# Eight residual sums held behind their written place, one addition per unit in the last batch, and the stores of routed rows sent one table after the other

## The chip, the cores and the metric

The kernel runs on one core of a Trainium2 chip. The core has four compute engines that each work through a queue of their own in order: TensorE (PE in the profile) multiplies matrices, VectorE (DVE) and ScalarE (ACT) work elementwise, GpSimd (POOL) adds and starts indirect transfers; SyncE (SP) starts the other transfers. The engines meet through semaphores. The metric is the device time of one execution in microseconds (us), and lower is better.

## The reference

Four blocks follow each other, each added to the residual `x` of 4 batches by 512 rows by 256 columns (fp32):

```python
x = x + _L0_xattn_ref(ctx_1024, _layernorm(x), ...)    # 8 heads of 128, keys: 1601 context rows and the 512 latents
x = x + _L0_ffn_ref(_layernorm(x), ...)                # 8 experts, top 2, capacity 512 rows per expert
x = x + _L1_xattn_ref(ctx_1024, _layernorm(x), ...)    # 8 heads of 32, keys: 1601 context rows, softmax
x = x + _L1_ffn_ref(_layernorm(x), W1, b1, W2, b2, Wr, br)

def _L1_ffn_ref(x, W1, b1, W2, b2, Wr, br):            # 8 experts, top 2, no capacity
    logits = xf @ Wr + br
    topv, _ = lax.top_k(logits, TOPK)
    masked = jnp.where(logits >= topv[:, TOPK - 1:TOPK], logits, -jnp.inf)
    weights = jax.nn.softmax(masked, axis=-1)
    h = gelu(jnp.einsum('td,edh->eth', xf, W1) + b1[:, None, :])
    expert_out = jnp.einsum('eth,ehd->etd', h, W2) + b2[:, None, :]
    return jnp.einsum('etd,te->td', expert_out, weights)
```

The softmax of the second attention needs, for each query and head, the sum of its 1601 exponentials. The last block routes each row to two of eight experts.

## The kernel before

The four blocks are four stages on the time line. The first attention ends at about 1600 us, the first FFN at 1883, the second attention at 2416, and the second FFN at the end of the span.

**The order of work.** Instructions are written in one program, and a scheduler orders each engine's queue by its own priorities, unless the program ties it: `tc.keep_in_program_order(instruction)` ties one instruction to its written place in its engine's queue, and `in_order(*computing)` ties all of PE, VectorE, ScalarE and GpSimd. The whole second attention is tied so (line 1753); the end of the first FFN is not.

**The end of the first FFN.** It works in two halves of eight experts (`all_experts`). Beside the second half, `keys_next` projects the context of batch 1 to the keys and values of the second attention: PE writes `ps_k` (L1166) and `ps_v` (L1182), and VectorE and ScalarE copy them to the tile `kv` in turn (`evacuate`, L122 and L124). After the ninth of these steps `add_collected(0, got0)` adds the FFN's results to `x` of batch 0: GpSimd has fetched eight tiles `g` of 128x256 from the table `slot_y` by indirect transfers (L360), and VectorE adds each, times its share (L382). The layer norm of batch 0 (statistics L143 and L144) follows. Here the scheduler chose the order: all eight sums and the statistics stand in VectorE's queue ahead of the copy of the last 65 columns of keys, "L122 kv<-ps_k 128x65".

**The second attention.** It has 16 units: four batches, two groups of four heads (`o`), two halves of 256 queries (`f`); units 12 to 15 are the last batch. A unit has seven steps (`PER_UNIT`) of 256 keys, the last one shorter. A global step (0 to 111) takes these in turn: `weights` of this step (PE L1538 and L1548, then four exponentials by ScalarE, L1562, into two tiles `pT` of 128x1024); then, for the step before, `weigh` (PE L1581 multiplies `pT` by the values), `add_weights`, the `maxima` of the next unit (PE L1281, VectorE's reduction "tops" L1292, in seven rotating PSUM banks that `weights` uses too), and `total`. Sums of exponentials are made in one of two ways. For a step in `ADDED = (1, 3, 5)` VectorE adds its two tiles to those of step 0 (L1571), and at the last step PE multiplies these sums by ones (L1600). For the other steps PE multiplies `pT` itself by ones in `total` (L1600, 16 matmuls). At the end of a unit, `closing` scales the outcome (VectorE, L1628 and L1630, to the tile `got`, of which there is one) and GpSimd adds it to `x` (L1637).

**Routing for the second FFN.** While batch b+1 is in the attention, `route2(b)` (L440 to L617) prepares batch b for the last stage, cut into pieces that are put at fixed steps (`routed`, `last_routed`): the layer norm, the tile `pay` (four tiles of 128 normalised rows with their number and shares; for batches 0 to 2 GpSimd writes it, L455 and L463, and there is one such tile), its transposes by PE (L194), the router's logits, the two experts of each row and the places of its rows. There are two tables in the chip's memory: `rows_a` holds the first G = 256 rows of each expert among batches 0 to 2, `rows_b` all that come after. A row whose place is in the other table is given a place out of bounds, which the transfer drops. So every tile of 128 rows is sent four times: for each of its two experts (k) to `rows_a` and to `rows_b`, by indirect stores of GpSimd (`scatters`, L591): 16 stores per batch, alternating between the tables, two at a time, at steps 56 to 63 for batch 0, 84 to 91 for batch 1, and 105 to 111 for batch 2. Batch 3, which has only the eight stores to `rows_b`, is routed in the last stage. Stores to the same table are ordered by a semaphore: the next one waits until the one before has landed. The pay of batch 2 is at step 92, its transposes at steps 93 and 94.

**The start of the second FFN.** At step 109 SP loads the first expert's rows from `rows_a` to `cw` (`load_first_rows`, L1677); at step 111 PE transposes them (`turn_first`, L1483), and the first expert's first layer follows (L1492). Then come, in the last stage, the layer norm of batch 3 (L143), which needs all additions to `x`, the load of the second expert's rows (L1829), their transposes (L1483), VectorE's copy of these (L1484) and the second expert's matmuls (L1492).

Of the kernel before, what the change touches and what calls it, by code (L numbers as in the profile page):

```python
# [11 lines left out]
AF = mybir.ActivationFunctionType  # L12
ALU = mybir.AluOpType
# [5 lines left out]
B, S, D = 4, 512, 256  # L19
M = 1601  # L20
NT = S // P
# [27 lines left out]
NOWHERE = 65536.0  # L49
PER_UNIT = -(-NM // 2)  # L50
ADDED = (1, 3, 5)

# [28 lines left out]
def xattn_ffn_twice(ctx: ExitStack, tc: tile.TileContext, a: dict, out: bass.AP):  # L83
    nc = tc.nc
# [128 lines left out]
    rows_a = dram.tile([E * G, PAY], F32, name="rows_a")  # L213
    rows_b = dram.tile([ROWS + G, PAY], F32, name="rows_b")
# [154 lines left out]

        return got, [lambda t=t, k=k: one_of(t, k) for t in range(NT) for k in range(2)]  # L370

    def add_collected(b, got, tiles=range(NT), by=None):
        for t in tiles:
            for k in range(2):
                j = b * NT + t
                xs = x[b][:, t, :]
                g, share = got[2 * t + k], prob[k][:, j : j + 1]
                if by:
                    by.tensor_scalar(g, g, share, None, ALU.mult)
                    by.tensor_tensor(xs, xs, g, ALU.add)  # L380
                else:
                    nc.vector.scalar_tensor_tensor(xs, g, share, xs, ALU.mult, ALU.add)  # L382


    lane_i = brief.tile([P, 1], I32, name="lane_i")
# [18 lines left out]
    place_a = [const.tile([P, NX], I32, name=f"place_a{k}") for k in range(2)]  # L404
    place_b = [const.tile([P, NX], I32, name=f"place_b{k}") for k in range(2)]
# [31 lines left out]
    def route2(b, two, psum, tag, first=0, n=NT):  # L437

        by = nc.vector if b == B - 1 else nc.gpsimd
# [144 lines left out]
        def scatters():  # L584

            sent = 0
            for k in range(2):
                for t in range(n):
                    for rows, at in ((rows_a, place_a), (rows_b, place_b))[b == B - 1 :]:
                        j = b * NT + first + t  # L590
                        nc.gpsimd.indirect_dma_start(  # L591
                            out=rows[:, :],
                            out_offset=bass.IndirectOffsetOnAxis(ap=at[k][:, j : j + 1], axis=0),
                            in_=pay[:, t, :],
                            in_offset=None,
                            bounds_check=E * G - 1 if rows is rows_a else ROWS - 1,
                            oob_is_err=False,
                        )
                        sent += 1
                        if sent % 2 == 0:  # L600
                            yield

        sending = scatters()
        for t0 in range(0, n, 2):
            ps = psum.tile([P, 2, D], F32, tag=tag, name="ps_b2")
            for k in range(2):
                t = t0 + k
# [3 lines left out]
            xs = xb[:, t0 : t0 + 2, :]  # L611
# [6 lines left out]
        yield from sending  # L618


    banks, tags = {}, {}

    def slots(of, e, half, n=CT):
# [705 lines left out]
    with ExitStack() as st:  # L1329
# [117 lines left out]
        def keys_next():  # L1447
            *kv, steps = keys_values(ps_s, "s", 1)
            kvs.append(kv)
            steps[9:9] = [lambda: add_collected(0, got0)]  # L1450
            steps = iter(steps)
            asking = queries(0, qTs)

            for few, asks in ((4, 0), (5, 0), (3, 1), (0, 1), (2, 1), (0, 1), (1, 1), (1, 1), (0, 1)):
                for _ in range(few):
                    next(steps)()
                for _ in range(asks):
                    next(asking)
                yield
            assert next(steps, None) is None  # L1460

            firsts = [(0, g) for g in range(len(pieces))] + [(1, g) for g in range(3)]
            for k, (u, g) in enumerate(firsts):
                maxima(u, g)
                if (u, g) == (0, len(pieces) - 1):
                    negated(0)
                yield
                if k == 0:
                    next(asking)
                    assert next(asking, None) is None  # L1470
                if (u, g) == (1, 0):
                    to_row(0)
                if k % 2 == 0:
                    yield
# [34 lines left out]
    with ExitStack() as st:  # L1509
# [20 lines left out]
        def weights(u, s):  # L1530

            b, o, f = units[u]
            js = keys_of(s)
            r, n = rows_of(js[-1], NM, TAIL), len(js) * QH
            pss = [ps_s.tile([P, 512], F32, tag="s", name=f"ps_w{i}") for i in range(HG)]
            for i in range(HG):
                rows = slice(i * DH1, i * DH1 + 2 * PARTS)
                nc.tensor.matmul(  # L1538
                    pss[i][:r, :n].rearrange("p (k q) -> p k q", q=QH),
                    lhsT=ones_b[rows, :r],  # L1540
                    rhs=below[u % 2][rows, :].unsqueeze(1).to_broadcast([2 * PARTS, len(js), QH]),
                    start=True,
                    stop=False,
                )
            for k, j in enumerate(js):
                for i in range(HG):
                    rows = slice(i * DH1, (i + 1) * DH1)
                    nc.tensor.matmul(  # L1548
                        pss[i][:r, k * QH : (k + 1) * QH],
                        lhsT=kvs[b][0][o][rows, j * P : j * P + r],  # L1550
                        rhs=qTs[b][rows, o, f * QH : (f + 1) * QH],
                        start=False,
                        stop=k == len(js) - 1,
                    )
            pTs = []
            for h in range(2):
                if s == 0:
                    pT = two.tile([P, 2, 512], F32, tag=f"sum{h}", name=f"sum{h}")
                else:
                    pT = some.tile([P, 2, 512], F32, tag="pT", name="pT")  # L1560
                for i in range(2):
                    nc.scalar.activation(pT[:r, i, :n], pss[2 * h + i][:r, :n], AF.Exp)  # L1562
                pTs.append(pT)
            if s == 0:
                sums[u] = pTs
            return pTs

        def add_weights(u, s, pTs):
            if s in ADDED:
                for to, pT in zip(sums[u], pTs):  # L1570
                    nc.vector.tensor_tensor(to, to, pT, ALU.add)  # L1571

# [16 lines left out]

        def total(u, s, pTs, ps):  # L1590

            of = [(s, pTs)] if s and s not in ADDED else []
            if s == PER_UNIT - 1:
                of.append((0, sums.pop(u)))
            for s0, tiles in of:
                js = keys_of(s0)
                r = rows_of(js[-1], NM, TAIL)
                for k in range(len(js)):
                    for i in range(HG):
                        nc.tensor.matmul(  # L1600
                            ps[i * DH1 : (i + 1) * DH1, QH:],
                            lhsT=ones[:r, :DH1],
                            rhs=tiles[i // 2][:r, i % 2, k * QH : (k + 1) * QH],
                            start=False,
                            stop=s0 == 0 and k == 1,
                            skip_group_check=True,
                        )
# [601 lines left out]
```

## Time and profile before

| quantity | value |
|---|---|
| median of 3 runs | 2722.71 us (2721.53, 2722.71, 2730.08) |
| the profiled execution | 2712.06 us, its span 2710.2 us |
| mean granted clock of TensorE | 0.991 |
| end of the exponentials (L1562) of step 56, 59 | 2160.18, 2176.15 us |
| of step 84, 86, 91 | 2298.61, 2307.96, 2331.05 us |
| of step 105, 107, 111 | 2397.29, 2404.45, 2414.20 us |
| start of unit 12, 13, 14, 15 | 2293.48, 2325.92, 2360.19, 2393.93 us |
| landing of the last store of batch 0, 1, 2 | 2193.30, 2330.86, 2423.76 us |
| half of TensorE's clock granted | 1750.19 to 1760.43, 2378.24 to 2388.48 us |

The span runs from the first to the last instruction of the profiled execution, and all times of the profile count from its start. The execution's own time has 1.9 us more than the span. The lines of the profile read: start, length, engine, line of the program, operation, output from inputs with their shapes, how many instructions are put together, and in square brackets the idle time of the engine before it and what ended it. A store's length on GpSimd (about 1 us) is that of issuing it; its landing is later, 2.07 to 3.72 us after its start for those whose landing the trace has in the second attention.

### The profile page before, as it was taken

How to read it: one execution, taken by the hardware profiler on the slowest of the kernel's cores; microseconds unless marked ns; L12 is line 12 of the kernel's file. 1: busy time of each engine (PE TensorE's matmuls, PEld its weight loads, DVE VectorE, ACT ScalarE, POOL GpSimd, SP SyncE). 2: the span in 40 equal slices, each digit the busy share in tenths (PEclk: the TensorE clock that was granted, in tenths of full speed). 3: DMA queues.
4: the chain of work that ended last, by engine and by line, in shares of the span. 5: the costliest groups of instructions: out<-in, count | busy, mean ns of one | idle time of the engine just before them, and what ended most of it. 6: DMA issues, size and time to landing. Idle time of an engine off the chain costs nothing. (4 is left out here: it accounts for less than half of the span.)

```text
span 2710.2 us, 38196 instructions
## 1 busy us (share of the span) xinstructions
PE 2636.0 (97%) x14620; PEld 1790.7 (66%) x14620; DVE 1364.6 (50%) x2461; ACT 917.9 (34%) x1577; POOL 356.9 (13%) x372
## 2 busy tenths in 40 slices
PE   6999999999999999999999999899999999999997
PEld 3666676666666666767666678777454454468887
DVE  6544556644456544455454441124777878853111
ACT  4332234333334233333333221122444444452221
POOL 0000000100000100000100000101441431322542
PEclk9999999999999999999999999999999999999999
DMA  5444434433443443433343455543433100025672
GB/s 178 111 113 121 99 90 113 105 93 89 108 112 84 115 98 85 99 95 87 98 104 95 124 184 166 177 156 99 125 123 122 64 30 7 20 98 180 202 222 78
DMA packets 191323, 302.89 MB, mean 112 GB/s; under 512 B 41783, under 2 KB 113272, under 8 KB 188440
## 3 DMA queue, kind: packets, MB, share of 16 engines
q1 hardware_dynamic: 152392, 218.33, 29.0%
q0 software_dynamic: 14160, 46.31, 5.8%
q10 hardware_dynamic: 24576, 35.68, 5.2%
q8 instruction: 118, 1.93, 0.3%
q14 instruction: 77, 0.63, 0.1%
HBM read 111.46 MB, written 51.07 MB: 60 GB/s over the span
## 5 line engine op out<-in xcount | busy, mean ns | idle before, releaser
L949 DVE TENSOR_REDUCE top<-ps_s 128x1 f32<-128x2113 f32 x128 | 301.7, 2357 | 584.1 <-PE ps_s L941 584.1
L978 PE MATMUL ps_o<-pT,v 128*128 128x256 f32 x2176 | 519.4, 380 | 0.0
L941 PE MATMUL ps_s<-kT,qT 128*128 128x512 f32 (+1 forms) x1280 | 489.1, 526 | 6.3 <-ACT attn L955 6.3
L978 PEld LDWEIGHTS ps_o<-pT,v 128*128 128x128 f32 x2176 | 407.9, 190 | 110.5 <-issue 65.4
L955 ACT ACTIVATE attn<-ps_s,top 128x2113 f32<-128x2113 f32 x128 | 259.0, 2024 | 478.4 <-DVE top L949 458.8
L941 PEld LDWEIGHTS ps_s<-kT,qT 128*128 128x128 f32 x1280 | 241.8, 190 | 252.1 <-issue 236.0
L970 DVE STREAM_TRANSPOSE pT<-swapped 128x2176 f32<-128x2176 f32 x128 | 312.3, 2440 | 32.8 <-DMA swapped<-attn 23.4
L1292 DVE TENSOR_REDUCE tops<-ps_s 128x1 f32<-128x512 f32 (+2 forms) x428 | 251.1, 648 | 120.0 <-PE ps_s L1281 120.0
L887 PE MATMUL ps_k<-kvin,wkv 128*128 128x512 f32 (+2 forms) x640 | 259.4, 528 | 3.4 <-DVE kvin L807 2.9
L924 PE MATMUL ps_v<-wkv,kvin 128*128 128x256 f32 x1088 | 255.3, 381 | 1.9 <-ACT v L931 1.4
L924 PEld LDWEIGHTS ps_v<-wkv,kvin 128*128 128x128 f32 x1088 | 204.8, 190 | 38.3 <-issue 6.0
L1562 ACT ACTIVATE pT<-ps_w 128x512 f32<-128x512 f32 (+1 forms) x384 | 184.2, 565 | 130.9 <-PE ps_w L1548 130.8
L903 ACT ACTIVATE kT<-ps_k,bqk 128x512 f32<-128x512 f32 (+1 forms) x192 | 100.9, 555 | 259.6 <-PE ps_k L887 136.0
L887 PEld LDWEIGHTS ps_k<-kvin,wkv 128*128 128x128 f32 x640 | 115.8, 191 | 75.4 <-issue 64.0
L931 ACT COPY v<-ps_v 128x512 f32<-128x512 f32 x144 | 80.0, 560 | 213.2 <-PE ps_v L924 135.9
L1281 PE MATMUL ps_s<-kv,qT 32*128 32x512 f32 (+1 forms) x1024 | 128.4, 556 | 2.8 <-DVE got L1630 2.5
L1548 PE MATMUL ps_w<-qT,kv 32*128 32x256 f32 (+1 forms) x1664 | 119.2, 384 | 0.0
L1571 DVE TENSOR_TENSOR sum<-sum,pT 128x1024 f32<-128x1024 f32 x96 | 114.8, 1237 | 6.0 <-ACT pT L1562 6.0
L654 PE MATMUL ps_h<-sxT,w 128*128 128x256 f32 (+1 forms) x512 | 108.0, 367 | 4.0 <-DVE sxT L644 2.5
L741 POOL TENSOR_TENSOR x<-x,bo 128x256 f32<-128x256 f32 x16 | 11.7, 761 | 743.8 <-DVE lat L181 545.8
L1345 PE MATMUL ps_y<-w,hT 128*128 128x256 f32 x480 | 108.7, 382 | 0.0
L654 PEld LDWEIGHTS ps_h<-sxT,w 128*128 128x128 f32 x512 | 91.8, 190 | 21.1 <-issue 4.2
(317 smaller groups left out, 2763.0 us busy)
## 6 DMA issues: line engine op xcount, KB each, us to landing
swapped<-attn SPq DMA_DIRECT2D x1536, 68.0 KB, 2.1
swapped<-attn ACTq DMA_DIRECT2D x512, 68.0 KB, 2.3
w<-in_w_dram SPq DMA_DIRECT2D x32, 1024.0 KB, 5.8
rows_b<-empty SPq DMA_DIRECT2D x36, 530.0 KB, 4.6
w_e<-in_wall_dram SPq DMA_DIRECT2D x5, 2052.0 KB, 11.2
cw<-in_ctxT_dram SPq DMA_DIRECT2D x4, 1601.0 KB
ctx_b<-in_ctx_dram SPq DMA_DIRECT2D x3, 1536.0 KB, 7.6
slot_x<-scrap SPq DMA_DIRECT2D x8, 512.0 KB, 3.3
```

What stands on the lines that cost most here:

```text
L654: nc.tensor.matmul(ps[:, f, :], lhsT=w1[:, c, (f0 + f) * P : (f0 + f + 1) * P], rhs=sxT[:, c, :], start=c == 0, stop=c == DC - 1,)
L887: nc.tensor.matmul(ps[:, :n], lhsT=wkv[:, c, hs], rhs=kvin[:, c, : n // 32, k, :] if k < 4 else flat_kvin[c][:, left : left + P], start=c ...
L924: nc.tensor.matmul(ps[:, k, :], lhsT=flat_kvin[c][:, j * P : (j + 1) * P], rhs=wkv[:, c, cols], start=c == 0, stop=c == DC - 1,)
L941: nc.tensor.matmul(flat[:, j0 : j0 + n], lhsT=qT[:, t * P : (t + 1) * P], rhs=kT[:, j0 : j0 + n], start=True, stop=True,)
L949: nc.vector.tensor_reduce(top, flat[:, :L], AX.X, ALU.max, negate=True)
L955: nc.scalar.activation(attn[:, :L], flat[:, :L], AF.Exp, bias=top, accum_out=total)
L970: nc.vector.transpose(pT[:, :, k * P : (k + 1) * P].rearrange("p c (a i) -> p a c i", a=4), swapped.rearrange("p a (c i) -> p a c i", i=32),)
L978: nc.tensor.matmul(ps, lhsT=v[:, j - parts[part][0], (h % 2) * DH0 : (h % 2 + 1) * DH0], rhs=pT[:, j, :], start=j == 0, stop=j == NB - 1,)
L1281: nc.tensor.matmul(pss[i][:, at : at + n], lhsT=qTs[b][rows, o, q0 : q0 + P], rhs=kvs[b][0][o][rows, j0 : j0 + n], start=True, stop=True,)
L1292: nc.vector.tensor_reduce(tops[u][:, t : t + at // n, some, j0 // 512], of, AX.X, ALU.max,)
L1548: nc.tensor.matmul(pss[i][:r, k * QH : (k + 1) * QH], lhsT=kvs[b][0][o][rows, j * P : j * P + r], rhs=qTs[b][rows, o, f * QH : (f + 1) * Q ...
L1562: nc.scalar.activation(pT[:r, i, :n], pss[2 * h + i][:r, :n], AF.Exp)
```

## The change

It has three parts.

The eight sums of `add_collected(0, got0)` are tied to their written order (`behind=True`). In the changed order VectorE has the copy of the 65 columns of keys, two copies `sxT` of the FFN and the first two copies of values ahead of the first sum; seven sums stand ahead of the third copy of values.

For the units of the last batch the steps whose `pT` VectorE adds are `ADDED_LATE = (3,)`. Sixteen additions of 128x1024 leave VectorE's queue (steps 1 and 5 of four units), and eight blocks of matmuls with ones (L1600) join PE's.

The stores of a batch go to `rows_a` first, all eight, and then to `rows_b`, at the same steps as before. Each store has another wait: for the last exponential of the step in which it is written (`latest[0]`). On GpSimd's queue the addition L1637 of the unit that closes among the stores stands after the sixth store of `rows_a` for batches 0 and 1, and after the eighth for batch 2. SP's load of the first expert's rows, which stood behind the sixth store of batch 2 to `rows_a` with the last two held until it had ended, now stands behind the eighth.

```diff
@@ -49,6 +49,7 @@
 ADDED = (1, 3, 5)
+ADDED_LATE = (3,)
@@ add_collected @@
-    def add_collected(b, got, tiles=range(NT), by=None):
+    def add_collected(b, got, tiles=range(NT), by=None, behind=False):
 ...
-                    nc.vector.scalar_tensor_tensor(xs, g, share, xs, ALU.mult, ALU.add)
+                    summed = nc.vector.scalar_tensor_tensor(xs, g, share, xs, ALU.mult, ALU.add)
+                    if behind:
+                        tc.keep_in_program_order(summed)
@@ route2, scatters @@
-            for k in range(2):
-                for t in range(n):
-                    for rows, at in ((rows_a, place_a), (rows_b, place_b))[b == B - 1 :]:
+            for rows, at in ((rows_a, place_a), (rows_b, place_b))[b == B - 1 :]:
+                for k in range(2):
+                    for t in range(n):
                         j = b * NT + first + t
-                        nc.gpsimd.indirect_dma_start(
+                        store = nc.gpsimd.indirect_dma_start(
 ...
+                        tc.add_manual_dep(
+                            store.ins,
+                            latest[0].ins.name,
+                            mybir.DependencyInfo(
+                                mybir.DependencyClass.Sync, mybir.DependencyReason.DATA
+                            ),
+                            reason="paced",
                         )
                         sent += 1
@@ before the stages @@
+    latest = []
@@ keys_next @@
-            steps[9:9] = [lambda: add_collected(0, got0)]
+            steps[9:9] = [lambda: add_collected(0, got0, behind=True)]
@@ weights @@
-                    nc.scalar.activation(pT[:r, i, :n], pss[2 * h + i][:r, :n], AF.Exp)
+                    latest[:] = [
+                        nc.scalar.activation(pT[:r, i, :n], pss[2 * h + i][:r, :n], AF.Exp)
+                    ]
@@ add_weights and total @@
+        def added(u):
+            return ADDED if units[u][0] < B - 1 else ADDED_LATE
+
-            if s in ADDED:
+            if s in added(u):
 ...
-            of = [(s, pTs)] if s and s not in ADDED else []
+            of = [(s, pTs)] if s and s not in added(u) else []
```

More of the change, by code (lines that the diff above doesn't have):

```diff
@@ L597, in scatters @@
                             oob_is_err=False,
+                        )
+                        tc.add_manual_dep(
[5 more added lines that the diff above has]
+                            reason="paced",
                         )
```

## The prediction, made before the change was run

> **What bounds the kernel now.** I read the page's busy shares first, then the windows of the two stretches that the diff touches, then waits and timelines there.
>
> ```profile
> PE 2636.0 (97%) x14620; PEld 1790.7 (66%) x14620; DVE 1364.6 (50%) x2461; ACT 917.9 (34%) x1577; POOL 356.9 (13%) x372
> ```
>
> TensorE is busy for 97%: a change gains only what it takes from PE's idle time (74 us) or half-clock stretches, and costs whatever keeps PE waiting. First the end of the first FFN, by timeline (start, length, engine, line, idle before it and releaser):
>
> ```profile
> 1752.94 0.48 DVE L382 SCALAR_TENSOR_TENSOR x<-g,prob,x 128x256 f32<-128x256 f32 x1 [1.76 <-DMA g<-slot_y,slot]
> 1754.21 0.22 DVE L122 COPY kv<-ps_k 128x65 f32<-128x65 f32 x1
> 1754.49 12.70 PE L1182 MATMUL ps_v<-cw 128*128 128x256 f32 x44 [6.41 <-DVE kv L122]
> ```
>
> PE stands 6.41 us for a 0.22 us copy, because that copy is queued on VectorE behind the residual sums, which wait for gathers. By windows (PE, PEld, DVE, ACT, POOL busy, then clock, DMA share, GB/s) the clock falls with it, and again in the last batch:
>
> ```profile
> 1752.00:1754.00 2.00, 0.00 (x0) 0.00 (x0) 1.03 (x4) 0.00 (x0) 0.00 (x0) 0.50 0.12 42
> 1758.00:1760.00 2.00, 2.00 (x6) 1.58 (x5) 0.69 (x1) 0.00 (x0) 0.00 (x0) 0.50 0.00 0
> 2293.50:2325.90 32.40, 30.06 (x375) 15.21 (x371) 27.65 (x59) 14.79 (x31) 13.10 (x13) 1.00 0.12 40
> 2325.90:2360.20 34.30, 30.98 (x393) 16.04 (x389) 27.38 (x61) 15.80 (x35) 10.32 (x11) 1.00 0.02 6
> 2360.20:2393.90 33.70, 30.50 (x355) 15.43 (x347) 26.14 (x75) 14.96 (x32) 3.58 (x4) 0.85 0.02 6
> 2460.00:2480.00 20.00, 20.00 (x95) 16.50 (x94) 3.28 (x9) 5.16 (x13) 4.64 (x5) 1.00 0.66 207
> ```
>
> The third to fifth rows are units 12 to 14: VectorE is busy for about 80%, yet PE lacks only 2.3, 3.3 and 3.2 us. The last row shows the second FFN bound by PE alone, so a late start there isn't won back. The waits in units 12 to 14 (total, times, longest):
>
> ```profile
> PE ps_w L1538 <- DVE tops L1292: 8.1, 14, 1.5
> POOL pay L455 <- DVE rs L177: 10.7, 1, 10.7
> ```
>
> Last, GpSimd's timeline of the stores of batch 2, with the work that follows them on SP and VectorE:
>
> ```profile
> 2389.97 1.08 POOL L591 DMA_INDIRECT rows_a<-pay,place_a  x1 [8.82 <-DVE place_b L573]
> 2391.35 0.98 POOL L591 DMA_INDIRECT rows_b<-pay,place_b  x1 [0.30 <-issue]
> 2393.10 1.63 POOL L591 DMA_INDIRECT rows_a<-pay,place_a  x1 [0.77 <-DMA rows_a<-pay,place_a]
> 2396.71 0.98 POOL L591 DMA_INDIRECT rows_a<-pay,place_a  x1 [0.70 <-DMA rows_a<-pay,place_a]
> ...
> 2421.12 0.97 POOL L591 DMA_INDIRECT rows_b<-pay,place_b  x1 [0.50 <-DMA rows_b<-pay,place_b]
> 2424.91 0.72 POOL L1637 TENSOR_TENSOR x<-x,got 128x256 f32<-128x256 f32 x1 [2.83 <-DVE got L1630]
> 2425.67 0.75 DVE L143 BATCH_NORM_STATS2 st<-x 128x6 f32<-128x256 f32 x2 [0.42 <-POOL x L1637]
> 2426.42 0.66 DVE L1484 COPY xT<-tp 128x512 f32<-128x512 f32 x1
> 2427.18 7.14 PE L1492 MATMUL ps_h<-xT,w_kv 128*128 128x256 f32 x32 [0.17 <-issue]
> ```
>
> A store waits for the landing of the one before it to the same table; two chains run side by side, one of each table. After the last store comes GpSimd's last addition of unit 15, then the layer norm of batch 3, and behind that in VectorE's queue the copy that PE needs.
>
> **Part 1, the residual sums behind their written place.** In the changed order the 65-column copy, two sxT copies and two copies of values come ahead of the eight sums. Removed: the 6.41 us wait, and the half clock, which lasts 10.24 us of which PE works 5.94 (1754.49 to 1760.43), so 2.97 us are lost to it. Together -9.4. What is late next: the third copy of values stands behind seven sums. Values come at 1.73 us per tile, and the last gather's sum could start at 1752.94 before; so these sums (0.48 each, 3.8 with their statistics) end by about 1759, and PE needs that bank at about 1761.7. Cover 2.7 us; if it is gone, up to 6.4 returns. Gain between 6.4 and 10; I take 9.4.
> The Trainium skill ("TensorE: Matmul & The Clock Gate", Why this matters for your kernels) says that no gap over some 3 us should be left between bursts, one idle window of 3.4 us halving the clock, and 3.4 us of work bringing it back. Here it stayed half for 5.94 us of work, and by the rule's figure 1.7 us rather than 2.97 would be lost.
>
> **Part 2, one addition per unit in the last batch.** Sixteen DVE additions of 128x1024 go (two in a row take 2.35 us at 2324.81, so 4.7 us per unit). Eight blocks of 16 matmuls with ones come; a block at 2355.08 takes until the next matmul at 2356.09, 1.0 each, so +8.2 in PE's own time. PE's waits behind the eight places sum to 8.4 us, and all idle time in units 12 to 14 is 8.9. Net 0, between -4 (most waits already go with fewer additions) and +8 (none go). The half-clock stretch of 2378.2 to 2388.5, which follows waits of under 1.6 us each, costs about 4.5 and may go or be replaced: I take -3.
>
> **Part 3, stores to one table in a row.** Each store waits for its predecessor's landing, now with no second chain beside it. The price is the period from start to start. Where a landing released the store, rows show 2.71 (2398.72 to 2401.43, rows_b), 2.73, 2.75, 3.13 and 3.61 (the first two pairs of rows_a above). The quietest landing took 2.07 us plus 0.27 to the next start, 2.34; the same kind of store in the first FFN's chain has 2.53 to 3.7, median 3.3. I take 2.7, as nothing of the other table runs beside; ends 2.34 and 3.3.
> The Trainium skill ("DMA: Bandwidth & Descriptors", Anatomy of one DMA) gives about 2.0 us plus bytes by 436 GB/s; for 132.5 KB that is an estimate of 2.3, 2.57 with the restart, which would put the end shift below at about +13. It also speaks against such a chain, since most of the time is a receipt that nothing overlaps.
> The pace: a store waits for the last exp of its step. Within a chain this is met; it delays only the heads. Queued behind a waiting store on GpSimd are the additions L1637 and the next batch's pay (L455), which also needs the last landing.
> *Batch 0*: exps of step 56 end at 2160.18, of 59 at 2176.15, so the last landing is about 2210, and pay needs the tile at 2210.56 with 3.8 us to PE's need: 0 (0 to +3).
> *Batch 1*: two stores from 2298.6, the third at the exps of step 86, 2308.0; five periods of 2.85 (landings were slower here, 2.33 to 3.67), 1.3 to the other table, seven periods and a landing of 2.6: 2346.2. Pay started at 2338.88 and took 8.0 to the transposes at 2346.89, where PE had 0.4 us to spare. So pay is 7.3 late, from which some DVE-side waits after it, and the later arrival of PE by part 2, take 2: a stall of 5 to 6, plus half clock as at 1754, about +3. Ends: +1 by 2.34, +11 by 3.3. I take +8, so with the -3 of part 2, +5 at this point.
> *Batch 2*: t0 is the end of the exps of step 105, 2397.29; before, the first store was 7.3 earlier. From t0: 0.3, fourteen periods (37.8), 2.0 from the last store of rows_a over the addition L1637 to the first of rows_b, 2.6 to land, 0.4: 43.1. The layer norm was at t0 + 28.4. Shift +14.7 (by 2.34: +9; by 3.3: +23.5). SP's load of the first rows, which waits for the eighth rows_a store, comes at about t0 + 21.5, its transposes stood at t0 + 16.6: a stall of some 5 that lies within the shift. PE then idles for some 10 us more, so half clock as at 1754: +3 (0 to 4).
>
> **Sum.** -9.4 + 5 + 14.7 + 3 = +13.3 on the profiled execution's 2712.06 (span 2710.2): 2725.4. That execution is 10.65 below the median of 2722.71 (2721.53 to 2730.08); I forecast against the median: 2736.
>
> **The rivals.** (1) *Short chain, no change*: period 2.34 throughout. -9.4, batch 1 +1 with part 2's -3 to 0, batch 2 +9, clock +1: -1 to +2, 2723. For it: landings of 2.07 and 2.22 where traffic is low. Against: five of the periods above.
> (2) *Faster*: the second FFN doesn't depend on the last store, VectorE's copy for PE being ahead of the layer norm, and the part 2 relief counts in full. Place: units 12 to 15; price -9.4, -4.5 of the half clock, -2.7 (8.9 idle less 6.2 of new blocks in three units), +3 for batch 1: -13.6, 2709. It decides where both delays of the stores sum to less than 1.2 us; the end shift is nil only below a period of 1.7, under every row. Against it too: the 0.66 us copy stands behind the layer norm in the queue.
> (3) *The gap only moves*: the third copy of values waits for gathers that are late. 6.4 comes back: 2742.
> (4) *The pace does nothing*, the heads of the chains going out as before: 7.3 of the shift of batch 2 falls away: 2729. Against: the exps of step 105 end 7.3 us after the first store of before started, and the wait is on them.
>
> **How the numbers follow.** Forecast with its neighbours 2731 to 2748, among them (3) at 0.1: 0.71. Rival (1) and (4): 0.2. Rival (2): 0.09. Within 0.3%, 8 us, a measurement of this kernel doesn't tell a change from none. The low end takes rival (1) with -10 in part 1 and -4.5 of the half clock against +1 and +9, which is 2718; the high end the 3.3 period at batch 2 without its clock term and half of batch 1's excess, +26: 2749. Slower 0.70, same 0.21, faster 0.09.
>
> **What would show it.** Step 1: no idle time over 1 us ahead of L1182, clock 1.0 at 1750 to 1760. Step 2: waits of L1538 on tops below 4 us in units 12 to 14, units no shorter than before by over 1 us. Step 3: stores to one table at 2.5 to 3.0 us, the wait of pay now on a DMA, PE idle for over 4 us ahead of L194; the last rows_b store about 41 us after the exps of step 105; PE idle some 15 us in sum between the first rows' load and L1492 of the second expert. Wrong if stores come at under 2.3 us, or PE finds work while the last of them land.

## The result, and the profile after

The changed kernel takes 2726.22 us (median of 20 runs, 2722.78 to 2732.67), the kernel before beside it 2721.85 (20 runs): a ratio of 1.0021, 95% interval 1.0013 to 1.0029, slower by 3.5 to 7.9 us. The time lies in the forecast range and on the forecast side; the forecast rise of 13.3 us was 1.7 to 3.8 times the measured one. The profiled execution has a time of 2723.88 and a span of 2722.2, which is 12.0 above the span of the profiled execution of before. The medians say +4.4 and the profiles +12.0; the experiments below ask why the two differ.

TensorE's row of the page:

```profile
PE 2639.2 (97%) x14748; PEld 1791.9 (66%) x14748; DVE 1345.5 (49%) x2445; ACT 918.7 (34%) x1577; POOL 352.0 (13%) x372
```

PE has 128 more matmuls for 3.2 us more of busy time, and the span is 12 longer: it waits more. At the end of the first FFN (timeline) it does not; the lines of the changed program stand 1 to 17 lower than those of before:

```profile
1744.07 11.41 PE L1194 MATMUL ps_v<-cw 128*128 128x256 f32 x52
1751.19 0.69 DVE L123 COPY kv<-ps_v 128x512 f32<-128x512 f32 x1 [2.77 <-PE ps_v L1194]
1751.80 1.39 DVE L383 SCALAR_TENSOR_TENSOR x<-g,prob,x 128x256 f32<-128x256 f32 x3
```

The 52 matmuls run through, the sums start when VectorE's second copy of values is done, and nothing waits for them. The next rows are the windows of before's ten us with half clock, and of four stretches after it: steps 84 to 92, the transposes of batch 2, steps 105 to 110, and the start of the second FFN.

```profile
1750.00:1760.00 10.00, 10.00 (x64) 8.82 (x63) 6.84 (x20) 2.54 (x7) 0.31 (x1) 1.00 0.02 6
2281.60:2320.30 38.70, 36.77 (x474) 17.85 (x467) 29.18 (x68) 16.86 (x35) 11.79 (x12) 1.00 0.11 36
2320.30:2342.80 22.50, 14.35 (x186) 7.32 (x182) 8.26 (x21) 7.09 (x15) 10.75 (x14) 0.84 0.05 14
2386.40:2405.70 19.30, 19.30 (x302) 12.22 (x302) 4.37 (x6) 12.63 (x25) 5.43 (x6) 1.00 0.12 40
2405.70:2440.00 34.30, 19.31 (x133) 13.30 (x133) 4.59 (x26) 7.35 (x16) 11.75 (x13) 0.77 0.21 61
```

Two rows have PE idle and the clock down: 8.15 us without a matmul in the third row, 15 in the last. The first of them in the timeline:

```profile
2333.50 0.97 POOL L594 DMA_INDIRECT rows_b<-pay,place_b  x1 [1.51 <-DVE tops L1304]
2336.19 1.23 POOL L458 TENSOR_SCALAR pay<-x,mv,rs 128x256 f32<-128x256 f32 x1 [1.73 <-DMA rows_b<-pay,place_b]
2337.48 0.47 PE L195 MATMUL tp<-ident,pay 128*128 128x128 f32 x1 [4.32 <-POOL pay L458]
2339.13 0.47 PE L195 MATMUL tp<-ident,pay 128*128 128x128 f32 x1 [1.18 <-POOL pay L458]
2342.41 0.48 PE L195 MATMUL tp<-ident,pay 128*128 128x128 f32 x1 [1.17 <-POOL pay L458]
```

The last store of batch 1 lands, pay is written, and PE waits four times for it, 7.8 us in all. The second, the stores of batch 2 and what stands behind them:

```profile
2390.53 1.08 POOL L594 DMA_INDIRECT rows_a<-pay,place_a  x1 [14.09 <-ACT oT L1630]
2393.65 0.98 POOL L594 DMA_INDIRECT rows_a<-pay,place_a  x1 [2.05 <-DMA rows_a<-pay,place_a]
...
2410.50 0.98 POOL L594 DMA_INDIRECT rows_a<-pay,place_a  x1 [1.39 <-DMA rows_a<-pay,place_a]
2412.41 0.99 POOL L594 DMA_INDIRECT rows_b<-pay,place_b  x1 [0.17 <-issue]
2412.66 1.76 SPq L1694 DMA_DIRECT2D cw<-rows_a  x4
2414.96 0.45 PE L1495 MATMUL tp_f<-ident,cw 128*128 128x128 f32 x1 [6.71 <-DMA cw<-rows_a]
...
2433.81 0.97 POOL L594 DMA_INDIRECT rows_b<-pay,place_b  x1 [1.83 <-DMA rows_b<-pay,place_b]
2436.69 0.75 DVE L144 BATCH_NORM_STATS2 st<-x 128x6 f32<-128x256 f32 x2 [7.30 <-DMA rows_b<-pay,place_b]
2437.45 0.66 DVE L1496 COPY xT<-tp 128x512 f32<-128x512 f32 x1
2438.20 4.04 PE L1504 MATMUL ps_h<-xT,w_kv 128*128 128x256 f32 x10 [7.05 <-DVE mv L145]
```

Each chain of eight runs at one landing after the other, 2.85 us per store to `rows_a` and 3.06 to `rows_b` on average. PE waits 6.71 us for the first rows and 7.05 for the second expert, and the latter begins 11.0 later than before. These waits were forecast. What the pair of profiles cannot say is why 20 runs of each kernel show only a third of these 12 us.

### The profile page after: what moved, and what is told of

It reads as the page before. It is cut to its first block, busy times and chain, and to the rows that moved or that the text cites. A ratio compares the mean times of both kernels' runs of the same rounds, so it can differ in the third digit from the quotient of the medians.

```text
span 2722.2 us, 38454 instructions
## 1 busy us (share of the span) xinstructions
PE 2639.2 (97%) x14748; PEld 1791.9 (66%) x14748; DVE 1345.5 (49%) x2445; ACT 918.7 (34%) x1577; POOL 352.0 (13%) x372
## 5 line engine op out<-in xcount | busy, mean ns | idle before, releaser
L1357 PEld LDWEIGHTS ps_y<-w,hT 128*128 128x128 f32 x480 | 90.2, 190 | 14.9 <-issue 2.4
```

What stands on the lines that cost most here:

```text
L1357: nc.tensor.matmul(ps[:, t, :], lhsT=hT[:, f, t * P : (t + 1) * P], rhs=w2[:, f, :], start=f == 0, stop=f == FC - 1,)
```

## The experiments

Distances between two profiles below are those of the same matmul's start. "Steps 84 to 92" is the time from the first weight load of line L1538 of step 84 to that of step 92, in which ten stores of batch 1 go out in before, and so for others; "rest" runs from that of step 111 to the end of the last matmul. "The first profile" is that of before which the prediction read. The kernels were run in five sets, each on one chip, with the kernel before timed beside them in each. "Full-clock span" is span times mean granted clock: the clock in the traces is either whole or half, so the product counts half-clock time by half. The clock is on record to 0.001, which is 2.7 us of such a span.

**First set: before again, and each part alone on the kernel before.** The diffs of the parts are those of the change, cut to the part; part 3 is the new order of the loops with the wait on `latest[0]`.

> The kernel before, unchanged, with a profile of its own and its span and granted clock execution by execution. My theory: the steps of the prediction are right in the profiled pair (span 2710.2 to 2722.2, +12.0), and what was wrong is the base: the profiled execution of before was one at the low end, so typical executions of it lie some 10 us higher, at a granted clock near 0.988 instead of 0.991, the excess being time at half clock. Then these executions show spans of 2713 to 2728 that fall in a line with the clock, and a new profile has a half-clock stretch more than the first. Rival: the spread has nothing to do with the clock (gathers and stores that land later), then spans of 2718 to 2722 come at a clock of 0.991.

> The residual sums tied to written order, on the kernel before, nothing else. My theory: the 6.41 us wait and the half clock behind it go: -9 to -11 us, that is a ratio of 0.9960 to 0.9967. Rival (the gap only moves to the third copy of values): -3 us. Second rival (in typical executions the clock had stayed full through that gap): -6.

> One addition per unit in the last batch, on the kernel before. My theory: the eight blocks cost 8.2 us and save as much in waits: 0, and -4 with the half-clock stretch of units 13 and 14 gone, which the profiled pair suggests (the distance fell by 4.2 us between 2348 and 2387). Rival (VectorE bounds the last batch): -8 to -12.

> The stores to one table in a row, paced, on the kernel before. My theory by the profiled pair: a stall of 4 to 6 us at the transposes of batch 2 with half clock behind it (+8) and +18 to +20 at the start of the second FFN: +24 to +28 against the profiled execution. If the executions of before lose time at half clock that these stalls replace, less: +15 to +20 in the medians. Rival (stores hidden): 0 to +5.

| kernel | median us | ratio to before, 95% | steps 56-64 | 84-92 | 92-98 | 98-105 | 105-111 | rest |
|---|---|---|---|---|---|---|---|---|
| before, first profile | | | 40.7 | 38.6 | 28.0 | 33.7 | 18.3 | 284.2 |
| before again | 2720.71 | 0.9996 (0.9985 to 1.0007) | 44.2 | 45.9 | 28.0 | 33.7 | 19.7 | 284.6 |
| part 1 alone | 2714.02 | 0.9974 (0.9965 to 0.9984) | 42.8 | 45.6 | 28.0 | 33.2 | 18.5 | 287.9 |
| part 2 alone | 2720.21 | 1.0000 (0.9987 to 1.0012) | 41.6 | 50.7 | 28.0 | 28.1 | 27.2 | 285.6 |
| part 3 alone | 2741.81 | 1.0078 (1.0064 to 1.0092) | 40.7 | 39.1 | 38.3 | 30.1 | 18.3 | 307.1 |
| changed kernel | 2726.22 | 1.0021 (1.0013 to 1.0029) | 40.7 | 38.7 | 38.5 | 27.5 | 19.2 | 303.5 |

Kernels with the old stores took 7 to 12 us longer in steps 84 to 92 than the first profile, those with the new ones did not. So part of my expectation fell, and its rival held: what typical executions lose is not half clock (before again has a clock of 0.991, as the first profile). The window of steps 84 to 92 in before again, where the same work takes 7.3 us more and PE is idle for 6.3 us instead of 3.4:

```profile
2295.70:2341.60 45.90, 39.60 (x439) 18.56 (x431) 34.03 (x71) 17.34 (x36) 14.12 (x14) 0.96 0.10 32
```

Its timeline there:

```profile
2321.22 1.23 PE L1548 MATMUL ps_w<-qT,kv 32*128 32x256 f32 x16
2324.26 0.60 ACT L1562 ACTIVATE pT<-ps_w 128x512 f32<-128x512 f32 x1 [4.09 <-PE ps_o L1581]
...
2325.82 0.97 POOL L591 DMA_INDIRECT rows_b<-pay,place_b  x1 [0.30 <-issue]
...
2327.84 0.60 ACT L1562 ACTIVATE pT<-ps_w 128x512 f32<-128x512 f32 x1 [0.77 <-remote]
2328.63 0.97 POOL L591 DMA_INDIRECT rows_b<-pay,place_b  x1 [0.30 <-issue]
2329.27 0.64 PE L1600 MATMUL ps_o<-pT,ones 128*32 128x256 f32 x5 [0.78 <-issue]
2330.83 2.48 DVE L1292 TENSOR_REDUCE tops<-ps_s 128x1 f32<-128x512 f32 x4 [5.41 <-remote]
```

Ten stores go out 1.3 to 2.0 us apart here, from 2315.8 to 2328.6. In their second half PE, ScalarE and VectorE all stand, then advance in small steps, released by nothing that the profile names ("remote", "issue"); 16 matmuls with ones take 5 us that take 1.07 elsewhere. GpSimd and its stores go on. I call this the stall.

Part 1 alone gains 4.4 to 9.5 us by its interval, below the 9 to 11 expected; its profile has the wait gone and the clock whole, and stands 10.5 ahead of the first profile at the start of the second attention, but only 7.4 ahead of before again. There the wait is nearly the same, and the half clock ends sooner, at 1756.09 instead of 1760.43, after 6.83 us (as it does in part 2 and part 3 alone):

```profile
1752.59 11.50 PE L1182 MATMUL ps_v<-cw 128*128 128x256 f32 x44 [6.31 <-DVE kv L122]
```

So 3.50 us of work fall into it, which cost 1.75 instead of 2.97, and part 1 can win some 8.1 in such an execution. Part 2 is worth nothing in the median: 98 to 105 fall by 5.6, and the stall comes in batch 2's stores as well (105 to 111 at 27.2). Part 3 costs 17 to 25. Summed, the parts give about +14, the change +4 to +8, so they don't add up. By the table, what part 2 gains in steps 98 to 105 is lost again to the stall in part 2 alone, and not in the changed kernel, which has 19.2 in steps 105 to 111. In part 3 alone PE waits at the two places of the changed kernel, longer at the first rows:

```profile
2428.78 0.45 PE L1492 MATMUL tp_f<-ident,cw 128*128 128x128 f32 x1 [11.64 <-DMA cw<-rows_a]
...
2451.21 4.15 PE L1501 MATMUL ps_h<-xT,w_kv 128*128 128x256 f32 x9 [6.33 <-DVE mv L144]
```

**Second set: the change without part 3, without the pace, without the order, and with the pace on two batches.** From the changed kernel:

```diff
 no_pace:   the call tc.add_manual_dep(store.ins, latest[0].ins.name, ...) taken out
 no_order:
-            for rows, at in ((rows_a, place_a), (rows_b, place_b))[b == B - 1 :]:
-                for k in range(2):
-                    for t in range(n):
+            for k in range(2):
+                for t in range(n):
+                    for rows, at in ((rows_a, place_a), (rows_b, place_b))[b == B - 1 :]:
 parts_1_2: both of these
 alternating_paced_0_1: as no_order, and
+                        if b < B - 2:
                             tc.add_manual_dep(
```

> The change without part 3: sums in written order and one addition per unit in the last batch; stores as before, alternating between the tables and unpaced. New theory: with the old stores, typical executions lose about 7 us in steps 84 to 92, where ten stores of batch 1 go out 1.3 us apart (38.6 us in the profiled execution of before, but 45.9, 45.6 and 50.7 in three others with the old stores, and 39.1 and 38.7 in two with the new ones), and 1 to 3 us in steps 56 to 64. So here steps 84 to 92 take 44 to 51 us, and the median gains only what part 1 gives: -7 (2711 to 2717). Rival (the excess in those steps is chance, not the stores): steps 84 to 92 at 38 to 41, and 2704.

> The changed kernel without the wait for the exponentials: one table after the other, each store on its predecessor's landing alone. If one store in flight at a time is what avoids the stall: steps 84 to 92 at 38 to 40 us, 56 to 64 at 40.7, and the chain of batch 2 begins about 7 us earlier than with the pace, so the end shift falls by 4 to 7: 2719 to 2722. If the pace avoids it: steps 84 to 92 at 44 or more, and 2726 or above.

> The changed kernel with the stores alternating between the tables as before, but each waiting for the exponentials of its step: two stores per step, four at most, and no long chain. If thin dense stretches suffice to avoid the stall: steps 84 to 92 at 38 to 40 us, no wait of PE at the transposes of batch 2, the second FFN within 4 us of its place in before: 2704 to 2709. If one store in flight is needed: steps 84 to 92 at 42 to 48: 2711 to 2717.

> As the one before, with only batches 0 and 1 paced: the stores of batch 2 start some 7 us earlier. If the stall is one of dense stores in any batch, steps 105 to 111 take 20 to 27 us here and 18 to 19 with the pace on all, and it is no better: 2705 to 2712. If it is confined to batch 1: 2701 to 2706.

| kernel | median us | ratio to before (2717.98), 95% | 84-92 | 92-98 | 98-105 | 105-111 | rest |
|---|---|---|---|---|---|---|---|
| parts 1 and 2 | 2706.81 | 0.9965 (0.9954 to 0.9976) | 46.1 | 28.0 | 28.0 | 24.9 | 285.1 |
| no pace | 2710.70 | 0.9971 (0.9959 to 0.9983) | 38.8 | 28.5 | 27.6 | 19.2 | 297.8 |
| no order | 2706.33 | 0.9968 (0.9956 to 0.9981) | 39.3 | 28.1 | 27.6 | 19.2 | 293.6 |
| alternating, 0 and 1 paced | 2703.97 | 0.9950 (0.9936 to 0.9963) | 39.3 | 28.1 | 28.1 | 23.2 | 285.1 |

In this set the profile of parts 1 and 2 has the stall, and either half of part 3 alone keeps it out of steps 84 to 92: the order, which leaves one store in flight, or the pace, which thins the stores. I had put the two as rivals; both hold. The times were less well forecast: parts 1 and 2 came out 4 us below their range and `no_pace` 8 below, and `no_order` lay in its range, but with a rest some 9 us above that of before, where at most 4 was expected. By the medians, keeping the stall out of steps 84 to 92 is worth less than these profiles show: parts 1 and 2 lie 2.8 above the kernel with two batches paced, and their profiled execution (2713.07) 6.3 above their own median.

Part 3 costs most when its halves come together. Against parts 1 and 2 the rest is 12.7 longer with the order alone, 8.5 with the pace alone and 18.4 with both, and only with both is the pay late (92 to 98 at 38.5 instead of 28). Without the pace the chain of batch 2 starts 15 us earlier by the clock of the span, and the kernel is 0.5% below the changed one (0.9971 against 1.0021, each beside before). What is left in `no_pace` is the last store:

```profile
2419.19 0.97 POOL L594 DMA_INDIRECT rows_b<-pay,place_b  x1 [1.74 <-DMA rows_b<-pay,place_b]
2422.01 0.75 DVE L144 BATCH_NORM_STATS2 st<-x 128x6 f32<-128x256 f32 x2 [9.48 <-DMA rows_b<-pay,place_b]
2423.52 2.90 PE L1495 MATMUL ps_h<-xT,w_kv 128*128 128x256 f32 x6 [9.23 <-DMA rows<-rows_a]
```

VectorE's layer norm waits for its landing, GpSimd's last addition having ended before that. Where only batches 0 and 1 are paced, the second FFN starts as in before (rest 285.1), and steps 105 to 111, with the dense stores of batch 2, cost 4 us again (23.2), as the first of the two expectations had it; the time is that of the second.

**Third set: the changed kernel again, and the start of the second FFN freed from the last store.** From the kernel without the pace:

```diff
+    pays.append(ctx.enter_context(tc.tile_pool(name="pays", bufs=1, side="right")))   # ahead of the second attention
-        pay = two.tile([P, n, PAY], F32, tag="pay", name="pay")
+        pay = (two if b == B - 1 else pays[0]).tile([P, n, PAY], F32, tag="pay", name="pay")
-            nc.gpsimd.tensor_tensor(
+            (nc.vector if u == len(units) - 1 else nc.gpsimd).tensor_tensor(
-        eight = st.enter_context(tc.tile_pool(name="d_eight", bufs=8))
+        eight = st.enter_context(tc.tile_pool(name="d_eight", bufs=7))
```

The tiles of the last stage then no longer take the memory of a pay that stores still read.

> The changed kernel, unchanged, beside the next one on one chip. Steps 84 to 92 at 38 to 40 us and 56 to 64 at 40.7 again, a wait of PE of 4 to 5 us at the transposes of batch 2, and waits of 6 to 7 us each at the first rows' transposes and at the second expert: 1.000 to 1.004 of before. If its profile had been a lucky one as that of before was: steps 84 to 92 above 43.

> The changed kernel without the pace, and with three edits that take the start of the second FFN off the last store: pay of batches 0 to 2 in a pool that lives on through the last stage, unit 15's addition to x by VectorE instead of GpSimd behind the stores, one buffer fewer in the pool of outputs (7 for 8, for the room). If the last store is what holds the second expert (PE stood 9.2 us there without the pace, with half clock after it): that wait goes, the rest after step 111 takes 285 to 288 us instead of 297.8, and the time is 2696 to 2702 on a chip where before has 2718. If another wait stands behind it, 2708 to 2712 as without the edits.

The changed kernel: 2723.48 against 2722.88, 1.0009 (1.0000 to 1.0018), with every stretch of its profile within 0.5 us of the first one. The freed end: 2699.47, 0.9913 (0.9899 to 0.9926), rest 286.5, as expected. Its timeline:

```profile
2413.74 0.74 DVE L144 BATCH_NORM_STATS2 st<-x 128x6 f32<-128x256 f32 x2
...
2415.57 7.07 PE L1496 MATMUL ps_h<-xT,w_kv 128*128 128x256 f32 x32
...
2425.19 0.97 POOL L594 DMA_INDIRECT rows_b<-pay,place_b  x1 [7.36 <-DMA rows_b<-pay,place_b]
```

The second expert starts 9.6 us ahead of the last store, without a wait. So it was the last store that held it. The row of `no_pace` names its landing, that is the pay's memory; GpSimd's addition behind the store was moved to VectorE in the same run, and the two were not run apart.

**Fourth set: the freed end with alternating stores, and with these spaced out.**

```diff
 freed_end_alternating: the loops in the order of before
 freed_end_spaced: that, and ahead of each store
+                        if b < B - 2:
+                            idle = two.tile([P, 32], F32, tag="idle", name="idle")
+                            for _ in range(8):
+                                nc.gpsimd.memset(idle, 0.0)
```

> The kernel with the freed end, with the stores alternating between the tables again and nothing else changed. What dense stores alone cost, where nothing waits for the last of them: steps 84 to 92 at 45 to 47 us instead of 38.7, 105 to 111 at 23 to 27 instead of 19.2, 56 to 64 at 42 to 44 instead of 40.7, less some 1.5 at the end: 0.9955 to 0.9975 of before, 10 to 16 us above the freed end. Rival (the stall isn't the stores' doing): 0.991 to 0.993.

> As the one before, with eight small writes by GpSimd to a spare tile ahead of each store of batches 0 and 1, so that its stores come some 2.5 to 3 us apart while they still alternate between the tables, two in flight. If it is the density of the stores: steps 84 to 92 back at 38 to 40 and 56 to 64 at 40 to 42, batch 2 as in the one before (105 to 111 at 23 to 27): 0.993 to 0.9955. If it is two tables or two stores in flight: steps 84 to 92 at 45 or more.

Both missed. Alternating: 2695.00, 0.9937 (0.9924 to 0.9951), steps 84 to 92 at 38.7 and 105 to 111 at 19.2, with the last eight stores of batch 1 within 10.2 us and no stall. Spaced: 2700.99, 0.9961 (0.9947 to 0.9974), 38.5, and also 19.2 in batch 2; PE waits three times at the transposes, 3.5 us in sum. So the spacing is not tested by this. But the kernel before had another time in this set, 2711.82, and full-clock spans with a median of 2686.2, against 2695.1, 2693.1 and 2694.0 in the three sets ahead of it. The first profile had 2686 too. So either moving the pay had cured the stall, or it had not been there in this set.

**Fifth set: before, the change and both freed kernels on one chip.** The four kernels are those above, unchanged.

> The kernel before, on the chip of the next three. By span times granted clock (the span as it would be at full clock, since the clock is either whole or half), before has 2695.1, 2693.1 and 2694.0 us in three sets of runs, but 2686.2 in the set of the last two kernels, and 2686 in the first profile. If the stall at the dense stores belongs to a set of runs (where program and data lie, or the chip) and not to the order of the stores alone: a set with 2693 to 2696 has steps 84 to 92 at 45 to 47 us here, a set with 2686 has 38 to 40.

> The changed kernel in the same set. Steps 84 to 92 at 38 to 40 us in any case. If the set has no stall in before: 12 to 14 us slower than before, as forecast (1.0045 to 1.0052). If it has: 1 to 6 slower (1.0004 to 1.0022).

> The freed end with alternating stores, again. If the stall belongs to the set: steps 84 to 92 as in before here, 45 to 47 or 38 to 40. If moving pay to another pool had removed it: 38.7 also where before has 45.

> The freed end with one table after the other, again: steps 84 to 92 at 38 to 39 us in any case, 2696 to 2700 at full speed of the second FFN's start. In a set without the stall, 1 to 4 us slower than the one before (a wait of PE of 1 to 3 us at the transposes of batch 2); in one with it, 6 to 10 us faster.

| kernel | median us | ratio to before (2710.92), 95% | 84-92 | 92-98 | 98-105 | 105-111 | rest |
|---|---|---|---|---|---|---|---|
| before | 2711.38 | 1.0000 (0.9990 to 1.0009) | 38.7 | 28.0 | 33.8 | 18.3 | 284.2 |
| changed kernel | 2724.40 | 1.0053 (1.0036 to 1.0069) | 38.5 | 38.5 | 27.6 | 19.2 | 303.1 |
| freed end, alternating | 2694.78 | 0.9937 (0.9921 to 0.9954) | 38.6 | 28.0 | 27.6 | 19.2 | 284.7 |
| freed end | 2699.66 | 0.9955 (0.9938 to 0.9971) | 38.5 | 28.6 | 27.6 | 19.2 | 285.8 |

Before has no stall here; the same window of steps 84 to 92:

```profile
2292.80:2331.50 38.70, 35.19 (x439) 17.37 (x431) 33.88 (x71) 16.86 (x35) 15.06 (x14) 1.00 0.11 38
```

As expected, the freed kernel with alternating stores is as before here, at 38.6. Whether moving the pay would cure the stall is not tested, as before has none in this set and, by its full-clock span, none in the fourth. The freed end is 4.9 us slower than the alternating one, where 1 to 4 was expected. The stall comes and goes with the set of runs, not with the program alone: the kernel before has 2721.8, 2718.0 and 2722.9 in three sets and 2711.8 and 2710.9 in two (its 2721.85 beside the first 20 runs of the changed kernel is of the higher kind). The full-clock spans hardly overlap: 2691.7 to 2698.6 over 38 executions of before in the first set, 2683.4 to 2692.2 over 32 in the fourth and fifth. It isn't the chip either, since the first and the fifth set ran on one chip, and the second and the fourth on another. The changed kernel takes 2726.2, 2723.5 and 2724.4 wherever it runs. So the change costs 13.5 us by the medians where before is undisturbed, as the steps of the forecast had it, and 0.6 to 4.4 where before is of the higher kind. In the first set the profiles show why: before again has the stall and the changed kernel has not. In the third set no profile of before was taken, and its full-clock span (2694.0) is the only sign. The freed end beats both kernels in both kinds of set (2699.47 and 2699.66).

## Why the prediction was right or wrong

**The steps.** In the fifth set, where both kernels are alike but for the change, the distances can be set against the terms of the sum. The cuts are the starts of steps 0, 96 and 104:

| term | forecast | measured, before to changed kernel |
|---|---|---|
| part 1 | -9.4 | -10.7 |
| batch 1: pay late, half clock | +8 | +8.7 |
| part 2, old half-clock stretch | -3 | -5.5 |
| batch 2: chain, half clock | +14.7 + 3 | +20.7 |
| sum | +13.3 | +13.2, less 0.6 at the start |

That the sums agree to 0.1 us is in part luck: the single terms miss by -1.3, +0.7, -2.5 and +3.0.

*Part 1* was right in mechanism and size, and rival (3) fell: the third copy of values was never late. Alone in the first set it gave 4.4 to 9.5 by the medians, less than the 10.7 of the pair, as the half clock behind the wait was shorter there. The second figure that the prediction had for the half clock, 1.7 us, is near the 1.75 of before again.

*Part 2* was right in mechanism: PE's waits on tops fell from 8.1 us to 2.7 in units 12 to 14, as the last section of the prediction had it (below 4). The changed kernel's line, of which the prediction shows the one before:

```profile
PE ps_w L1550 <- DVE tops L1304: 2.7, 7, 1.1
```

The blocks took the gain back, and what was won is about the half-clock stretch. This term was mis-sized: the prediction took 3 of a price of 4.5, and 5.5 was measured. Rival (2) fell on its condition: the second expert waits 7.05 us behind the last store.

*Part 3, batch 0* cost nothing, as said. *Batch 1*: the forecast stall of 5 to 6 was 7.8 in four waits (4.3 and three of 1.2), because PE waits for each of the four tiles of pay. The 0.4 us "to spare" was a misreading: in the row of 2346.89 PE already waits 0.43 us for pay, so nothing was to spare. *Batch 2*: the period was mis-sized. I took 2.7 on the ground that nothing of the other table runs beside; it measured 2.85 and 3.06, and fourteen of them are 3.6 us more. The estimate from the Trainium skill ("DMA: Bandwidth & Descriptors", Anatomy of one DMA), 2.3 and with this trace's restart 2.57, is further off still.

Rival (1) fell with it, as no chain had a mean near 2.34; that its 2723 lies nearer to the measured time than the forecast does is luck. Rival (4) fell as well: the heads of the chains wait for the exponentials, and taking that wait out was worth 0.5% across two sets, the pay of batch 2 and the start of the second FFN together.

**What failed** is the last step: "That execution is 10.65 below the median of 2722.71 (2721.53 to 2730.08); I forecast against the median: 2736." It carried the 10.65 over to the changed kernel, as if it were a property of the measurement. It was a property of the kernel before. Before again, whose time lies among the timed runs, has the stall in the stores of batches 0 and 1 (44.2 and 45.9 us instead of 40.7 and 38.6, 10.8 in sum, while +3.7 and -3.1 elsewhere nearly cancel); the profiled execution had not, and the change rewrites these stores (40.7 and 38.7). That the timed runs had the stall is inferred from this profile and their times; and in which set the first profile fell is not on record. So against the median part 3 had a gain of about 10.8, which the prediction put at nothing. The profiled execution lay below all three runs, by 9.4 us or more, which the text noted and didn't ask about. Against the profiled execution's own time the sum was 2725.4; the changed kernel measured 2726.2, and its own profiled execution lies 2.3 below its median. No rival had part 3 gain anything: the profile that I read shows ten dense stores without harm to any engine, so the gain could not be read from it.

**What stays open.** That the stall belongs to dense alternating stores is shown within two sets, by one profile of each kernel: all four kernels that have them in steps 84 to 92 there took 45.6 to 50.7, all four with the new order, the pace or both took 38.8 to 39.3. Why before is slower in three sets than in two, and what holds three engines while GpSimd goes on, is not settled. More traffic it is not: the DMA share is 0.10 in the window with the stall and 0.11 in the one without. Where program and tables lie in memory could differ from set to set; nothing here tests that. The spaced kernel ran in a set without the stall and says nothing on the density.

## What to carry to other kernels

Before a sum made on one profiled execution is carried to a median, ask what the difference between the two is and whether the change touches the work that could make it. An order that avoids a hazard may be worth little by itself if it hangs more on its last transfer: here the pace and the serial chain cost more than they saved, and taking the next stage off the last store (a buffer of its own for what the stores read, the last addition on another engine) took `no_pace` from 2710.70 to 2699.47 (each in its own set), below before in both sets in which it ran. Where a kernel's time moves by 0.4% from one set of runs to another, compare within a set, and profile the kernel before in it.

## What the runs showed of the hardware

- Ten indirect stores of 132.5 KB in a row, 1.3 to 2.0 us apart, can go with some 7 us in which PE, ScalarE and VectorE advance only in small steps (steps 84 to 92 at 45.9 us instead of 38.6), in some sets of runs and not in others. One at a time, 2.3 us apart or more within a table, no run had it; nor in pairs 3.1 us or more from pair to pair in batch 1; pairs 3.0 to 3.1 us apart went with 23.2 us instead of 19.2 in steps 105 to 111 (batch 2).
- A chain of such stores with one in flight at a time ran at 2.37 to 3.23 us per store (batch 2 of the changed kernel, means 2.85 and 3.06); with a second table's chain beside it, distances of 2.7 to 3.7 between stores to one table were seen (before, 2389.97 to 2401.43). So the single chain was little faster per store, and sixteen in a row took 43.3 us from first to last where the two chains took 31.2.
- Half-clock stretches that end within the span have lengths of 3.41, 6.83, 10.24 and once 13.65 us (part 3 alone), all multiples of 3.41. The Trainium skill ("TensorE: Matmul & The Clock Gate", Part 1) tells of windows of about 3.4 us, which agrees. After one and the same wait of 6.3 to 6.4 us the half clock lasted 10.24 us in one profile and 6.83 in another. A stretch of 10.24 also followed waits of no more than 1.53 us each (before, at 2378.24); the changed kernel, with those waits at 1.1 or less, has none there.
